# A graph network on one core: the attention of layer 2 is turned back a slot earlier, and its denominators by transposes

## The chip, the cores and the metric

The kernel runs on one core of a Trainium2 chip. A core has five engines that work through queues of their own: TensorE (PE; its weight loads are shown as PEld), VectorE (DVE), ScalarE (ACT), GpSimd (POOL) and SyncE (SP), which issues most of the transfers. Engines wait for each other by semaphores, and an instruction that waits holds up everything behind it on its engine. TensorE writes its results to PSUM, a small memory of banks; another engine must read a bank before TensorE may use it for something else. The metric is the device time of one execution in microseconds (us). Three runs of the kernel before took 2074.66, 2077.97 and 2079.85 us; the median is 2077.97.

## What is computed

Four layers of graph network over 32 graphs of 512 nodes with 64 features. All graphs share one adjacency matrix `adj`. Each layer normalizes, applies a relu, and adds its output to its input:

```python
h = jnp.maximum(_layernorm(x, axis=-1), 0.0)
x = x + _L0_gnn_ref(h, adj, w_self, w_neighbor, bias)   # h W + (adj h) W' + b
h = jnp.maximum(_layernorm(x, axis=-1), 0.0)
x = x + _L1_gnn_ref(h, 0, net_params, adj)              # twice: relu((adj z) W_i)
h = jnp.maximum(_layernorm(x, axis=-1), 0.0)
x = x + _L2_gnn_ref(h, adj, W, a)                       # attention, below
h = jnp.maximum(_layernorm(x, axis=-1), 0.0)
x = x + _L3_gnn_ref(h, adj, Wh, bh, W_out, b_out)       # eight heads and an output attention
```

The change is in layer 2, a graph attention:

```python
Wh = jnp.einsum('bnf,of->bno', h, W)
e = jax.nn.leaky_relu((Wh @ a[:F])[:, :, None] + (Wh @ a[F:])[:, None, :], negative_slope=0.2)
att = jax.nn.softmax(jnp.where(adj[None] > 0, e, NEG), axis=-1)
return jax.nn.elu(jnp.einsum('bij,bjo->bio', att, Wh))
```

## The kernel before

The batch is worked on in 16 pairs of graphs. A pair's values stand as 128 partitions by 512 elements: four blocks `c` of 128 nodes, two graphs `k`, 64 features. Layers 0 to 2 form the first stage, up to about 487 us; the rest of the time is layer 3, whose work is laid out in periods by `flow_period` and which the change leaves as it is, but for what the drain (below) runs ahead of it.

**Slots.** The first stage is a software pipeline written out by hand. `slot(k)` issues, for k from 0 to 16, layer 0 of pair k, layer 1 of pair k-2 and k-3, the preparation of layer 2 for pair k-4 and its attention for pair k-5 (the object `u`, of class `Gat`). The order of the calls is the order of the instructions on TensorE, VectorE and ScalarE, inside `tc.manual_schedule`. Within a slot, as it stands before the change:

- POOL adds the bias to x of pair k (L1122). ScalarE copies `nt1b`, a sum over neighbours that TensorE left in PSUM at the end of the slot before (`copied`, L928).
- VectorE adds `po0`, the projection of layer 0, to x (L1129) and centres the result for the next norm (`centre`: mean L861, L862, difference L863); ScalarE squares it (L881).
- TensorE sums over neighbours for layer 1 (`nt1`, L921) and transposes for the attention (`ht2`, L310); ScalarE copies both. VectorE makes half of the attention's scores (L1005). TensorE projects `nt1b` (`po1b`, L941), VectorE adds it with a relu (L1108).
- TensorE transposes (`ht0`) and sums (`nt0`) for layer 0, VectorE centres once more and makes the other half of the scores, TensorE projects `po1a` and prepares the next attention (`wh`, L967, and two `e1`, L974, whose exps into `c` are L990).
- A third centring; four variances (L899); TensorE multiplies the scores with the values, `acc` (L1018) and `den` (L1027), the latter as sums in 128 rows; ScalarE takes the roots (L906) and copies `acc` and `den` to SBUF, tile `kept` (L1037). VectorE weighs the next values (L995), takes reciprocals (L914) and finishes three norms (relu, L885).
- TensorE projects layer 0 (`po0`, L941) and sums over neighbours of `z` (L921, left in PSUM for the next slot). Then comes whatever `begun` has for this slot (`more`): in slots 6, 8, 10 and 12 the row checks `judge_rows` on VectorE (L201 to L213), in slot 15 `judge` (L240 to L244), which turns a column by TensorE.
- The end of the attention, `u.end()`: `read` multiplies `kept` with `pick`, a matrix of 128 x 2 that adds up two rows out of four sets (`den_ps`, L1049), turns the attention back by four transposes (`op_ps`, L1055), takes the reciprocal (L1060) and the product (L1062). `rest` takes the exp (L1070), adds into x (L1073, L1074), centres, and squares (L1076). Its variance is summed in the next slot (list `ended`).

The trace drops the digits of tile names: `nt0`, `nt1` and `nt1b` evacuate tiles that are all called `nt_ps`, and `ht0` and `ht2` both appear as `ht`.

ScalarE loads a table when it goes from a root to an exp or back (ACT_TABLE_LOAD). The load stands directly before the first instruction that needs it.

**Banks.** The first stage has three PSUM pools: `ps_t` with four buffers (neighbour sums, transposes, `wh`, `e1`, and before the change `op_ps` and `fill_ps`), `ps_o` with two (`po0`, `po1a`, `po1b`) and `ps_g` with two (`acc`, `den`, `den_ps`).

**The drain.** `drain` finishes the last four attentions, g2, g1, g0 and `last`, when no layer 0 is left to work beside them. `fill(n)` multiplies n times something that nobody reads. Before `last.scores(1)` it runs nine periods of `flow_period` ahead, which prepare layer 3's first features on ScalarE, transpose them (`hx_ps`) and multiply (`g_ps`).

Of the kernel before, what the change touches and what calls it, by code (L numbers as in the profile page):

```python
# [8 lines left out]
F32 = mybir.dt.float32  # L9
# [13 lines left out]
def fast_form(  # L23
# [818 lines left out]
    with (  # L842
# [107 lines left out]
        class Gat:  # L950
# [92 lines left out]

            def read(self):
                acc, tot = self.kept
                den = ps_g.tile([P, N], F32, name="den_ps", tag="acc")
                den = den[:, : 2 * C].rearrange("p (c k) -> p c k", k=2)
                for c in range(C):
                    nc.tensor.matmul(  # L1049
                        den[:, c], lhsT=tot[:, c * P : (c + 1) * P], rhs=pick,  # L1050
                        start=True, stop=True,
                    )
                op = ps_t.tile([P, C, 2, F], F32, name="op_ps", tag="ps")
                for c in range(C):
                    nc.tensor.transpose(  # L1055
                        op[:, c].rearrange("p k f -> p (k f)"), acc[:, c * P : (c + 1) * P],
                        ident,
                    )
                rec = tiny.tile([P, 2, C], F32, name="rec")
                nc.vector.reciprocal(rec.rearrange("p k c -> p c k"), den)  # L1060
                self.sq = o = work.tile([P, 2, C, F], F32, name="o")
                nc.vector.tensor_tensor(  # L1062
                    o, op.rearrange("p c k f -> p k c f"),
                    rec[:, :, :, None].to_broadcast([P, 2, C, F]), OP.mult,
                )
# [13 lines left out]
        n0, n1, n2, gat = {}, {}, {}, {}  # L1079
        ended = []  # L1080
        nt1b, z, po0 = {}, {}, {}
# [36 lines left out]
        def slot(k, more):  # L1118
# [15 lines left out]
            if n:  # L1134
                n.a()
                n.square()
                some.append(n)
            if l1:
                h = n1.pop(k - 2).h
                nt1 = copied(neighbours(lambda c: h[:, c]), "nt1")  # L1140
# [47 lines left out]
            if l0:  # L1188
                po0[k] = project([(ht0, ws2), (nt0, wn2)], "po0")
            if l1:  # L1190
                nt1b[k - 2] = neighbours(lambda c: z[:, c, :])
            if more:
                more()
            if u:
                u.end()

        def fill(n):


            p = ps_t.tile([P, N], F32, name="fill_ps", tag="ps")  # L1200
            for i in range(n):
                nc.tensor.matmul(p, lhsT=ident, rhs=adj_t[:, 0, :], start=True, stop=True)

        def drain():


            g2, g1, g0 = gat.pop(M - 4), Gat(M - 3, n2.pop(M - 3).h), None
            nt1b[M - 2] = copied(nt1b[M - 2], "nt1b")
            h = n1.pop(M - 1).h
            nt1 = copied(neighbours(lambda c: h[:, c]), "nt1")  # L1210
# [27 lines left out]
            g1.scores(0)  # L1238
            g0.flip()
            g2.read()  # L1240
            g1.scores(1)
# [12 lines left out]
            g2.rest()  # L1254
            g0.scores(0)
            g1.read()
            last.prepare()
# [7 lines left out]
            s = Spread()  # L1265
            s.add(g2)
            for i in range(-10, -1):
                flow_period(i)
            g0.read()
            last.scores(1)  # L1270
# [3 lines left out]
            g0.rest()  # L1274
            s.add(g1)
            last.read()
            last.rest()
# [9 lines left out]
        mask_t = setup.tile([P, C, N], F32, name="mask", tag="raw")  # L1287
        pick = setup.tile([P, 2], F32, name="pick")

        def edges():  # L1290
            nc.vector.tensor_scalar(mask_t, adj_t, 0.0, None, op0=OP.is_gt)
            nc.vector.tensor_tensor(
                pick, ident[:, 0::F], ident[:, 32::F], OP.add
            )

# [611 lines left out]
```

## Time and profile before

| | |
|---|---|
| runs | 2074.66, 2077.97, 2079.85 us; median 2077.97 |
| profiled execution | 2077.38 us, span 2075.5 us, mean granted clock 0.985 |
| TensorE busy | 1984.1 us (96%) |
| VectorE busy | 1746.2 us (84%) |
| ScalarE busy | 1319.3 us (64%) |
| POOL busy | 1446.3 us (70%) |
| slots 6 to 16 | 107.35 to 387.73 us |
| drain | 387.73 to about 487 us |

Times in the timeline are counted from the start of the span. A line of a timeline gives the start, the length, the engine, the source line, the instruction, what it writes and reads, and how many alike were merged; in brackets stands the idle time of the engine before it and what ended it. A line of a window gives the stretch, its length, then for TensorE, its weight loads, VectorE, ScalarE and POOL the busy time and the number of instructions, and then the clock that TensorE was granted (1.00 is full speed), the share of the transfers and GB/s. A matmul of float32 appears as two instructions, a transpose as one. Matmuls are pipelined, so the lengths of groups overlap a little; in the chain of waits, each step has only the time that it adds.

### The profile page before, as it was taken

The numbers are of one execution on the slowest core, as the hardware profiler recorded it, in microseconds if no ns is written. First come the engines' busy times: TensorE is split into PE (matmuls) and PEld (weight loads), VectorE is DVE, ScalarE is ACT, GpSimd is POOL, SyncE is SP. The second block draws the span as 40 slices with busy tenths as digits, with TensorE's granted clock in tenths as the row PEclk, the third lists the DMA queues.
The fourth block names the chain that finished last, engine by engine and source line by source line (L and its number), as shares of the span: only waits on it lengthen the run. The fifth ranks groups of instructions, "written<-read, shape, count | busy, mean of one in ns | idle before, by whom it ended". The sixth has DMA issues, their size and how long they took to land.

```text
span 2075.5 us, 29392 instructions
## 1 busy us (share of the span) xinstructions
PE 1984.1 (96%) x9438; PEld 744.5 (36%) x9438; DVE 1746.2 (84%) x4087; ACT 1319.3 (64%) x2008; POOL 1446.3 (70%) x834
## 2 busy tenths in 40 slices
PE   7999999877999999999999999999999999999995
PEld 4555555422333333333333333333333333333332
DVE  6688887647888998988888889888888888889994
ACT  3444444343676777677777777777777777776674
POOL 2000000002888999898989899998888988888996
PEclk9999999978999999999999999999999999999998
DMA  4000000000222223233323233232333233222233
GB/s 121 1 1 1 1 1 1 1 0 21 78 78 74 83 70 84 76 83 77 79 76 77 76 84 82 75 84 68 78 77 74 70 77 76 75 71 78 76 83 79
DMA packets 185875, 128.05 MB, mean 62 GB/s; under 512 B 124984, under 2 KB 130272, under 8 KB 185584
## 3 DMA queue, kind: packets, MB, share of 16 engines
q1 hardware_dynamic: 166480, 125.30, 22.9%
q10 hardware_dynamic: 18720, 0.59, 0.5%
q8 instruction: 76, 1.25, 0.3%
q14 instruction: 87, 0.71, 0.1%
q0 software_dynamic: 512, 0.20, 0.1%
HBM read 119.48 MB, written 5.37 MB: 60 GB/s over the span
## 4 chain that ended last, share of the span: by engine, by line
PE 78%; DVE 11%; POOL 5%; ACT 3%; DMA 2%; issue 2%; ACTq 0%; SPq 0%; DVEq 0%; POOLq 0%
PE s_ps L383 23%; PE av L438 21%; PE tot_ps L450 6%; PE y_ps L568 5%; PE gT_ps L613 5%; PE nt_ps L921 5%; POOL p_att L416 3%; PE g_ps L550 3%; PE acc L1018 2%; DVE s L1005 2%; PE den L1027 1%; DVE mean L861 1%; PE hx_ps L310 1%; PE po L941 1%; DVE p_att L395 1%
## 5 line engine op out<-in xcount | busy, mean ns | idle before, releaser
L416 POOL TENSOR_TENSOR p_att<-p_att,topb 128x1024 f32<-128x1024 f32 x429 | 1008.4, 2385 | 0.0
L395 DVE CUSTOM_DVE_ANT_0 p_att<-s_ps,flow_neg 128x512 f32<-128x512 f32 x1152 | 726.0, 686 | 100.0 <-PE s_ps L383 98.2
L383 PE MATMUL s_ps<-g,hx 64*128 64x512 f32 x2048 | 515.1, 614 | 14.0 <-DVE p_att L432 11.4
L420 POOL TENSOR_TENSOR p_att<-p_att,topb 128x512 f32<-128x512 f32 x286 | 360.7, 1284 | 170.9 <-DMA topb<-top_row 130.7
L429 ACT ACTIVATE p_att<-p_att 128x1024 f32<-128x1024 f32 x288 | 304.7, 1058 | 157.3 <-POOL p_att L420 77.0
L432 DVE TENSOR_TENSOR p_att<-e_ps,p_att 128x1024 f32<-128x1024 f32 x288 | 337.9, 1197 | 29.1 <-ACT e_ps L429 27.4
L429 ACT ACTIVATE e_ps<-p_att 128x1024 f32<-128x1024 f32 x288 | 292.6, 1029 | 74.0 <-POOL p_att L416 62.2
L383 PEld LDWEIGHTS s_ps<-g,hx 64*128 64x128 f32 x2048 | 174.9, 186 | 326.1 <-DVE top L395 174.8
L438 PE MATMUL av<-p_att,hd 128*64 128x512 f32 x1024 | 269.7, 605 | 0.2
L438 PE MATMUL av<-p_att,hn 128*64 128x512 f32 x1024 | 263.3, 592 | 0.0
L1122 POOL TENSOR_TENSOR x<-x,bias_b 128x512 f32<-128x512 f32 x16 | 20.4, 1279 | 296.1 <-DVE hn L863 296.1
L586 DVE SCALAR_TENSOR_TENSOR cat<-y_ps,bh,cat 128x512 f32<-128x512 f32 x256 | 180.1, 745 | 17.0 <-ACT cat L578 15.4
L562 ACT COPY g<-g_ps 128x512 f32<-128x512 f32 x128 | 131.8, 1138 | 91.3 <-PE g_ps L550 91.1
L578 ACT ACTIVATE cat<-y_ps,bh 128x512 f32<-128x512 f32 x256 | 161.3, 681 | 35.5 <-PE y_ps L568 35.2
L450 PE MATMUL tot_ps<-p_att,ones 128*32 128x512 f32 x1152 | 156.4, 608 | 3.7 <-DVE p_att L432 3.7
L568 PE MATMUL y_ps<-o_att,wh_sb 64*128 64x512 f32 x512 | 137.0, 594 | 0.0
L613 PE MATMUL gT_ps<-cat,wo_sb 128*64 128x512 f32 x512 | 131.6, 592 | 0.0
L438 PEld LDWEIGHTS av<-p_att,hn 128*64 128x64 f32 x1024 | 73.8, 137 | 146.0 <-issue 146.0
L438 PEld LDWEIGHTS av<-p_att,hd 128*64 128x64 f32 x1024 | 62.3, 136 | 165.5 <-issue 132.6
L921 PE MATMUL nt_ps<-adj_t,hn 128*128 128x512 f32 x256 | 117.0, 600 | 0.8 <-DVE hn L885 0.8
L487 DVE TENSOR_TENSOR o_att<-av,recb 128x512 f32<-128x512 f32 x144 | 99.1, 688 | 19.3 <-DMA recb<-rec_row 16.0
L528 POOL TENSOR_TENSOR hd<-hn 128x128 f32<-128x128 f32 x32 | 15.6, 487 | 138.5 <-ACT hn L519 138.5
(192 smaller groups left out, 2196.6 us busy)
## 6 DMA issues: line engine op xcount, KB each, us to landing
topb<-top_row SPq DMA_DIRECT2D x288, 256.0 KB
recb<-rec_row SPq DMA_DIRECT2D x288, 128.0 KB
out_dram<-y SPq DMA_DIRECT2D x32, 128.0 KB
x<-in_x_dram SPq DMA_DIRECT2D x3, 1024.0 KB
top_row<-top SPq DMA_DIRECT2D x144, 4.0 KB
parts<-tot SPq DMA_DIRECT2D x144, 4.0 KB
parts<-tot ACTq DMA_DIRECT2D x144, 4.0 KB
rec_row<-rec_flow SPq DMA_DIRECT2D x144, 4.0 KB
```

The lines of the kernel that those rows point to most:

```text
L383: nc.tensor.matmul(ps[:, k], lhsT=x[halves(k), r * P : (r + 1) * P], rhs=g[halves(k), :], start=True, stop=True,)
L395: nc.vector.tensor_tensor_reduce(out=self.p[r][:, k], in0=ps[:, k], in1=flow_neg[:, r], scale=-1.0, scalar=BIG, op0=OP.add, op1=OP.min, ac ...
L416: engine.tensor_tensor(self.p[r], self.p[r], self.topb, OP.subtract)
L420: engine.tensor_tensor(p, p, self.topb[:, k], OP.subtract)
L429: nc.scalar.activation(to, self.p[r], AF.Exp, scale=-1.0)
L432: nc.vector.tensor_tensor(self.p[r], self.joined, self.p[r - 1], OP.add)
L438: nc.tensor.matmul(self.av[halves(k), :], lhsT=self.v(k, j) if j % 2 else self.less_next(k, j), rhs=self.p[j][:, k], start=(j == 0), stop= ...
L450: nc.tensor.matmul(ps[q : q + 32, :], lhsT=ones, rhs=self.p[2 * e + 1][:, k], start=True, stop=True,)
L568: nc.tensor.matmul(ps, lhsT=wh_sb[halves(k), 2 * self.i + k, :], rhs=self.o[halves(k), :], start=True, stop=True,)
L586: nc.vector.scalar_tensor_tensor(self.cat[:, k], self.y[k], bh[:, h : h + 1], self.cat[:, k], op0=OP.add, op1=OP.max,)
L613: nc.tensor.matmul(self.gps[halves(k), :], lhsT=wo_sb[:, h, :], rhs=Heads.cat.pop((self.b + k, h)), start=(h == 0), stop=(h == H - 1),)
L921: nc.tensor.matmul(p, lhsT=lhs(k), rhs=adj_t[:, k, :], start=(k == 0), stop=(k == C - 1))
```

## The change

`read` is split. A new method `back` does its work on TensorE: four transposes of the denominators (instead of four multiplications with `pick`) into `den_ps`, four of the attention into `op_ps`. `read` keeps the work of VectorE; since a transposed column holds each sum 32 times, it picks one of 32 and adds the two sets with a reduction, ahead of the reciprocal. In a slot, `back` is called directly behind the projection `po0`, ahead of the neighbour sums of `z`, and `end` (`read` and `rest`) is called in the next slot, behind the first centring and square. `op_ps` and `fill_ps` take their buffers from `ps_o` instead of `ps_t`. In the drain, `back` is called before each `read`, and for g0 both are called before the nine periods of `flow_period` instead of behind them.

```diff
-            def read(self):
+            def back(self):
                 acc, tot = self.kept
                 den = ps_g.tile([P, N], F32, name="den_ps", tag="acc")
-                den = den[:, : 2 * C].rearrange("p (c k) -> p c k", k=2)
                 for c in range(C):
-                    nc.tensor.matmul(
-                        den[:, c], lhsT=tot[:, c * P : (c + 1) * P], rhs=pick,
-                        start=True, stop=True,
+                    nc.tensor.transpose(
+                        den[:, c * P : (c + 1) * P], tot[:, c * P : (c + 1) * P], ident
                     )
-                op = ps_t.tile([P, C, 2, F], F32, name="op_ps", tag="ps")
+                op = ps_o.tile([P, C, 2, F], F32, name="op_ps", tag="po")
                 for c in range(C):
                     nc.tensor.transpose(
                         op[:, c].rearrange("p k f -> p (k f)"), acc[:, c * P : (c + 1) * P],
                         ident,
                     )
+                self.op, self.den = op, den
+
+            def read(self):
+                op, den = self.op, self.den
                 rec = tiny.tile([P, 2, C], F32, name="rec")
-                nc.vector.reciprocal(rec.rearrange("p k c -> p c k"), den)
+                den = den.rearrange("p (c k e r) -> p k c e r", c=C, k=2, e=2)
+                nc.vector.tensor_reduce(rec, den[:, :, :, :, 0], AX.X, OP.add)
+                nc.vector.reciprocal(rec, rec)
...
@@ slot @@
                 n.square()
                 some.append(n)
+            while turned:
+                turned.pop().end()
...
                 po0[k] = project([(ht0, ws2), (nt0, wn2)], "po0")
+            if u:
+                u.back()
+                turned.append(u)
             if l1:
                 nt1b[k - 2] = neighbours(lambda c: z[:, c, :])
             if more:
                 more()
-            if u:
-                u.end()
 
         def fill(n):
-            p = ps_t.tile([P, N], F32, name="fill_ps", tag="ps")
+            p = ps_o.tile([P, C, 2, F], F32, name="fill_ps", tag="po")
...
@@ drain @@
             nt1b[M - 2] = copied(nt1b[M - 2], "nt1b")
+            turned.pop().end()
...
+            g2.back()
             g2.read()
...
+            g1.back()
             g1.read()
...
             s.add(g2)
+            g0.back()
+            g0.read()
             for i in range(-10, -1):
                 flow_period(i)
-            g0.read()
             last.scores(1)
...
+            last.back()
             last.read()
```

`pick` and the instruction that made it are gone.

## The prediction

> **What bounds the kernel now.** I read the page's head and chain first, then the timeline of the three busy engines over one slot of the layer-0-to-2 stage, then the timeline of the drain, then the granted clock in 2 us windows.
>
> The page's head and its chain of waits:
>
> ```profile
> span 2075.5 us, 29392 instructions
> PE 1984.1 (96%) x9438; PEld 744.5 (36%) x9438; DVE 1746.2 (84%) x4087; ACT 1319.3 (64%) x2008; POOL 1446.3 (70%) x834
> PE 78%; DVE 11%; POOL 5%; ACT 3%; DMA 2%; issue 2%; ACTq 0%; SPq 0%; DVEq 0%; POOLq 0%
> ```
>
> From about 487 us on TensorE is the bound, and the change touches nothing there. Everything turns on the first 487 us, so the shares over the span say nothing. One slot there, on TensorE, VectorE and ScalarE (start, length, engine, line, instruction; in brackets the idle time before it and what ended it):
>
> ```profile
> 310.52 3.60 PE L921 MATMUL nt_ps<-adj_t,z 128*128 128x512 f32 x8
> 313.96 0.95 PE L1049 MATMUL den_ps<-pick,kept 128*128 128x2 f32 x8
> 314.77 0.63 PE L1055 MATMUL op_ps<-ident,kept 128*128 128x128 f32 x4
> 320.49 1.16 PE L941 MATMUL po1b<-wl,nt1b 128*128 128x128 f32 x8 [1.22 <-ACT nt1b L928]
> ...
> 314.94 0.21 DVE L1060 RECIPROCAL rec<-den_ps 128x8 f32<-128x8 f32 x1 [4.45 <-PE den_ps L1049]
> 315.44 0.69 DVE L1062 TENSOR_TENSOR o<-op_ps,rec 128x512 f32<-128x512 f32 x1 [0.28 <-PE op_ps L1055]
> 318.61 0.69 DVE L863 TENSOR_TENSOR o<-x,mean 128x512 f32<-128x512 f32 x1
> ...
> 309.38 1.28 ACT L1070 ACT_TABLE_LOAD   x1
> 316.16 0.63 ACT L1070 ACTIVATE e<-o 128x512 f32<-128x512 f32 x1 [5.50 <-DVE o L1062]
> 319.33 0.63 ACT L1076 ACTIVATE o<-o 128x512 f32<-128x512 f32 x1 [2.54 <-DVE o L863]
> 319.87 0.57 ACT L928 COPY nt1b<-nt_ps 128x512 f32<-128x512 f32 x1
> ```
>
> This is a ring. VectorE idles 4.45 us for `den_ps`, which stands behind `nt_ps<-z` on TensorE. Its five instructions of L1062 to L863 run 315.44 to 319.30; the square (L1076) follows; the `nt1b` copy stands behind the square on ScalarE's queue; `po1b` waits for the copy; from 320.49 TensorE works without a gap up to the next `op_ps`, 20.55 us. 20.55 + 5.07 = 25.62 us a slot. TensorE itself is busy 24.38 of them. Slots 6, 8, 10 and 12 end with row checks (L201 to L213) that run 284.36 to 289.59, 5.2 us of VectorE; they fit into the 4.45 us of idle but for 0.4. So two slots take 51.7 us.
>
> The drain, and the clock:
>
> ```profile
> 400.03 5.40 PE L921 MATMUL nt_ps<-adj_t,z 128*128 128x512 f32 x8 [1.93 <-ACT c L990]
> 418.01 2.07 PE L974 MATMUL e_ps<-ht,wa 64*128 64x512 f32 x2 [0.41 <-DVE o L1062]
> 437.65 1.81 PE L974 MATMUL e_ps<-ht,wa 64*128 64x512 f32 x2 [3.04 <-ACT c L990]
> 439.61 5.82 PE L1202 MATMUL fill_ps<-adj_t,ident 128*128 128x512 f32 x7
> 463.10 2.21 PE L310 MATMUL hx_ps<-ident,hs 128*128 128x128 f32 x8 [10.09 <-ACT hs L524]
> 467.98 1.86 PE L1049 MATMUL den_ps<-pick,kept 128*128 128x2 f32 x8
> ...
> 412.00:414.00 2.00, 1.67 (x16) 1.43 (x14) 1.90 (x5) 0.00 (x0) 0.00 (x0) 1.00 0.00 0
> 414.00:416.00 2.00, 0.42 (x8) 0.42 (x8) 2.00 (x4) 1.56 (x3) 0.00 (x0) 1.00 0.00 0
> 418.00:420.00 2.00, 1.99 (x2) 0.50 (x2) 2.00 (x4) 0.24 (x1) 0.00 (x0) 0.50 0.01 4
> ```
>
> `e_ps` waits 3.04 us for a bank, and `fill_ps` after it starts with VectorE's L1062 (438.86 to 439.55); both wait for buffers of the pool that also holds `op_ps`. Idles of 1.9 us (413.7 to 415.6) and 1.93 us (398.1 to 400.0) are each followed by a clock of 0.50, while the 1.66 us idle before `po1b` in the slots with row checks left it at 1.00.
>
> **The change, part by part.** T is the end of `nt_ps<-z` of the slot before; the times are laid end to end from the rows above and the like rows of that slot.
>
> *The matmuls of `pick`.* Eight passes, 0.79 us in the chain, become four transposes, priced like `op_ps` in the chain, 0.51 for four: -0.3 us a unit. Both sets now stand before `nt_ps<-z`, so TensorE needs 24.38 - 0.3 = 24.1 us a slot.
>
> *The extra reduction.* The nearest rows are L467 (128x8 from 128x16, 0.17 us) and L243 (from PSUM, 0.28). I take 0.2. In a slot VectorE then waits for the exp, which hides it; only the last unit pays it.
>
> *The move in an ordinary slot.* `po0` ends at T-4.4, VectorE's relu at T-4.2. The add of `po0`, mean, mean and difference run to T-1.9, the reduction, reciprocal, product and L1073 to T. Now the exp: on ScalarE it stands behind the `nt1b` copy (T to T+0.6), the square (to T+1.1) and its table load, which ran in an idle stretch before (309.38) and now runs behind the square, 1.28 us, to T+2.4; the exp ends at T+3.0. Behind it VectorE waits, and with it all its queue: L1074, means and difference to T+5.4, four scores to T+8.1, `po1b`'s two adds, means and difference to T+10.4. ScalarE's next square and the `nt0` copy end at T+11.5. The second `e1` matmul needs that copy for its bank and is reached by TensorE at T+11.3 (nt 3.44, ht 0.44, po1b 0.89, ht 0.44, nt 3.44, po1a 0.89, wh 1.04, e1 0.72). So the new chain just fits: 24.2 us, -1.4 against 25.62. Queued behind the exp on ScalarE are the square, the `nt1` and both `ht` copies; they end by T+7.6, and `po1a` wants `nt1` at T+8.6. The move issues no DMA and passes nothing on SP; POOL's bias add is ready some 7 us before its reader.
>
> *The move behind row checks.* The 5.2 us now have only T-4.2 to T before them and end at T+1.0. The add of `po0` starts there, the product ends at T+4.4, table load and exp at T+5.7, the difference at T+8.1, the scores at T+10.8, the second difference at T+13.1, the `nt0` copy at T+14.2. TensorE, at its second `e1` since T+11.8 (`po1a` too waits 0.4), idles 2.3 us, and a restart costs 0.3 (the first `po1b` above takes 1.16 us, in the chain 0.89): slots 7, 9, 11 and 13 take 26.7 us.
>
> *Slot 16.* VectorE waits in slot 15 for `own_ps` behind `nt_ps<-z` (365.21, hidden until now behind the same wait as `den_ps`). So it is as late, `nt1`'s copy stands behind the late square, `po1a` idles 3.9 us: 24.3 us against 22.2.
>
> *Sum of slots 6 to 16:* from `den_ps` at 107.35 to that at 387.73 are 280.4 us. After: 6 x 24.2 + 4 x 26.7 + 24.3 = 276.3, -4.1 us.
>
> *The clock.* The new idles of 2.3 and 3.9 us are longer than those that lost it. A loss costs 1.5 (`nt_ps` 5.11 us at 83.3 against 3.60) to 3.1 us (6.2 us at half from 418.0). Below: nothing, where the 2.3 us fall across two stretches. I take 2.2, midway, in three of the four slots, and in slot 16: +8.8. Slots: +4.7.
>
> On this the Trainium skill (TensorE: Matmul & The Clock Gate, "Why this matters for your kernels") advises against idle gaps above about 3 us. By it only slot 16 would lose the clock, and the total would be 6.6 us lower; the rows with 1.9 us decide.
>
> The Trainium skill speaks against the change in another place: ScalarE: Activation LUTs, "What ACT_TABLE_LOAD costs", puts a switch at 1.28 us for the load and 1.38 for a drain. By that the chain in every slot would be 1.4 us longer and the ordinary slot would gain nothing. Here the load at 431.69 is followed by the exp at 432.98 with nothing between, so 1.28 stands.
>
> *The drain.* (a) `nt_ps` at 400.03: its chain through the late exp gives about T+12.0 for T+12.4: -0.3. (b) `e_ps` at 418.01 no longer waits for L1062, and starts with the clock still up: -1.2. (c) `op_ps` and `fill_ps` leave `e_ps`'s pool: the wait of 3.04 and that for L1062 go, six fills run behind `e_ps` from 434.7, at full clock 5.2 us, to 439.9. Late next are the scores on VectorE (the last ends at 442.1, with the reduction 442.3): the last `acc` matmul and `den` (0.45 + 1.85) end at 444.7 for 453.06: -8.3. What hides it is nothing: after it comes a chain of single steps to 463.10. (d) The `den_ps` and `op_ps` at 467.98, 2.75 us to 470.8, move into the idle 10.09 us before 463.10: -2.75; I put back 0.4, since the clock at 0.50 until 475 may now reach into `acc`. (e) The last reduction +0.2. Sum -12.0; between -7 (the fills of (c) at half clock, 10 us) and -14 (`acc` in (b) and `nt_ps` in (a) at full clock).
>
> *Total:* 4.7 - 12.0 = -7.3. The profiled execution took 2077.38 us (2075.5 and 1.9 around it), 0.6 below the median of the runs, 2077.97. So 2070.1, and against the median 2070.7: I say 2070.5.
>
> **Rivals.** (R1) The clock holds through the stalls. For it: 1.66 us held. Against: 1.9 did not. Slots -4.1, drain -12.0: 2062.
>
> (R2) Slower: the half clock does not come back in the stalled slots. The work behind the second `e1` is half-width scores, `acc` and `den`; after 437.85 and 463.1 the clock took 7 and 12 us. Five places at p us each against 4.1 + 12.0: from p = 3.2 us on it is slower; with all of `acc`, `den` and `po0` at half (p about 7) 2097; at p = 4.6, midway, 2085. Against it: the time at half from 83 and from 400.3 was 3.4 us.
>
> (R3) The drain pays half: the fills run cold as they do now (439.61: 0.83 us each), and the late clock meets `acc`. -5 with slots +4.7: 2078.
>
> (R4) The change does not open the ring, since the exp is still behind other work. Then slots keep 51.7 us a pair: about 2066 with the drain alone.
>
> **How the numbers follow.** Likeliest case 0.46, with its own range 2066 to 2076; R1 0.18, R2 0.16, R3 0.14, R4 0.06. What a measurement can tell is 0.3%, 6.2 us: faster means below 2071.7, slower above 2084.2. Faster: 0.28 of the likeliest, all of R1, 0.05 of R4: 0.51. Slower: 0.11 of R2, 0.03 of R3, 0.01 of the likeliest: 0.15. Same: the other 0.34. The range takes in R1's centre and R2's turning point and a little more: 2060 to 2084.
>
> **What will show it.** Right: `po1b` without the 1.22 us idle; VectorE idle before L1078 by some 3 us, released by the exp; a table load behind the square; idle before `e_ps` behind row checks of about 2.3 us with a clock below 1.00 after it; the six fills starting right behind `e_ps`. Wrong: an ordinary slot above 24.5 us, a clock of 1.00 in slots 7 to 13, fills that still wait, or a start of the attention stage that moved by less than 3 us.

## The result and the profile after

The changed kernel took 2077.49 us (median of 12 runs, 2073.82 to 2080.06), the kernel before, on the same chip, 2077.55 (2074.66 to 2080.31). The ratio is 0.9999, with a 95% interval of 0.999 to 1.0008: no difference. One execution among the experiments (the exp behind the copy) took 2447.42 us at a mean granted clock of 0.781, where its four others had 0.980 to 0.985, and is left out of that kernel's ratio. The profiled execution took 2077.25 us, with a span of 2075.3 us and a mean clock of 0.981 (before: 2077.38, 2075.5, 0.985). The head and the chain of waits of the page after:

```profile
span 2075.3 us, 29298 instructions
PE 1984.9 (96%) x9374; PEld 738.2 (36%) x9374; DVE 1748.6 (84%) x4102; ACT 1320.3 (64%) x2008; POOL 1445.5 (70%) x834
PE 60%; POOL 6%; DMA 4%; DVE 3%; issue 1%; ACT 1%; SPq 0%; ACTq 0%; POOLq 0%; DVEq 0%
```

TensorE's total is as good as unchanged, and nothing in it says that the first 487 us were rearranged. The reading starts from the slots. The starts of the last neighbour sum of a slot, `nt_ps<-z`, give the length of each slot:

| slot | 6 | 7 | 8 | 9 | 10 | 11 | 12 | 13 | 14 | 15 | 16 | sum |
|---|---|---|---|---|---|---|---|---|---|---|---|---|
| before | 25.63 | 26.07 | 25.62 | 26.07 | 25.63 | 26.06 | 25.63 | 26.06 | 25.62 | 25.63 | 22.25 | 280.3 |
| after | 24.54 | 28.71 | 24.54 | 29.89 | 24.54 | 29.99 | 24.54 | 30.03 | 24.54 | 24.53 | 26.06 | 291.9 |

The ordinary slots became 1.1 us shorter. The four that follow row checks became 2.6 to 4.0 us longer, slot 16 by 3.8. Against that, the drain, from `nt_ps<-z` of slot 16 to the add behind the exp of g0, went from 98.4 to 80.8 us.

The changed kernel's timeline of TensorE, first a slot behind row checks (293.40 to 323.43), then an ordinary one:

```profile
308.18 1.07 PE L974 MATMUL e_ps<-ht,wa 64*128 64x512 f32 x2
311.18 2.07 PE L974 MATMUL e_ps<-ht,wa 64*128 64x512 f32 x2 [1.93 <-ACT nt L928]
313.18 5.71 PE L1018 MATMUL acc<-s,v 128*64 128x512 f32 x16
...
323.43 3.60 PE L921 MATMUL nt_ps<-adj_t,z 128*128 128x512 f32 x8
...
330.74 1.06 PE L941 MATMUL po1b<-wl,nt1b 128*128 128x128 f32 x8
...
337.43 1.07 PE L974 MATMUL e_ps<-ht,wa 64*128 64x512 f32 x2
338.71 1.12 PE L974 MATMUL e_ps<-ht,wa 64*128 64x512 f32 x2 [0.21 <-ACT nt L928]
339.77 3.65 PE L1018 MATMUL acc<-s,v 128*64 128x512 f32 x16
```

In the ordinary slot `po1b` (330.74) no longer waits. In its place the second `e_ps` waits for the `nt0` copy: 0.21 us. Behind row checks it waits 1.93 us, and what follows runs at half clock: the second `e_ps` takes 2.07 us for 1.12, `acc` 5.71 for 3.65.

VectorE and ScalarE of the same two slots, from the timelines of each engine:

```profile
297.58 0.68 DVE L1133 TENSOR_TENSOR x<-x,po 128x512 f32<-128x512 f32 x1
302.61 0.69 DVE L1078 SCALAR_TENSOR_TENSOR x<-e,x 128x512 f32<-128x512 f32 x1 [0.86 <-ACT e L1074]
...
322.83 0.69 DVE L1133 TENSOR_TENSOR x<-x,po 128x512 f32<-128x512 f32 x1 [3.30 <-PE po L941]
326.32 0.69 DVE L1077 SCALAR_TENSOR_TENSOR x<-o,x 128x512 f32<-128x512 f32 x1
330.15 0.69 DVE L1078 SCALAR_TENSOR_TENSOR x<-e,x 128x512 f32<-128x512 f32 x1 [3.14 <-ACT e L1074]
```

```profile
327.06 0.58 ACT L928 COPY nt1b<-nt_ps 128x512 f32<-128x512 f32 x1 [5.67 <-PE nt_ps L921]
327.55 0.63 ACT L881 ACTIVATE sq<-hn 128x512 f32<-128x512 f32 x1
328.20 1.28 ACT L1074 ACT_TABLE_LOAD   x1
329.49 0.63 ACT L1074 ACTIVATE e<-o 128x512 f32<-128x512 f32 x1
```

In the ordinary slot VectorE is done with L1077 at 327.0 and then waits 3.14 us for the exp. ScalarE has been idle for 5.67 us by then, but the `nt1b` copy, which waits for TensorE's last sums, stands ahead of the exp in its queue, and so do the square and the table load. Behind row checks VectorE starts at 297.58, 0.75 us after the end of those sums and not 4.0 us before it, as in the ordinary slot, and all that it does for TensorE comes later.

The drain, in TensorE's timeline of the changed kernel:

```profile
414.22 3.70 PE L921 MATMUL nt_ps<-adj_t,z 128*128 128x512 f32 x8 [2.82 <-ACT c L990]
428.09 1.11 PE L967 MATMUL wh_ps<-wgv,ht 64*128 64x65 f32 x16 [2.33 <-ACT ht L312]
...
430.04 2.84 PE L1210 MATMUL fill_ps<-adj_t,ident 128*128 128x512 f32 x6
...
442.00 5.42 PE L1210 MATMUL fill_ps<-adj_t,ident 128*128 128x512 f32 x12
```

The twelve instructions of `fill_ps` at 442.00 start right behind `e_ps` and take 5.42 us; before, they started after a wait of 3.04 us and ran cold. `nt_ps` takes 3.70 us for 5.40, and the six fills at 430.04 take 2.84: in this execution the clock was kept, although the waits ahead of them are long (2.82 us, before the change 1.93, and 2.33). In the second profile of the changed kernel (below) it was lost at this `nt_ps`, which took 6.55 us behind the same wait. Layer 3's first L395 starts at 487.12 us, 2.85 us earlier than before.

### The profile page after: what moved, and what is told of

It reads as the page before. It is cut to its first block, busy times and chain, and to the rows that moved or that the text cites. A ratio compares the mean times of both kernels' runs of the same rounds, so it can differ in the third digit from the quotient of the medians.

```text
span 2075.3 us, 29298 instructions
## 1 busy us (share of the span) xinstructions
PE 1984.9 (96%) x9374; PEld 738.2 (36%) x9374; DVE 1748.6 (84%) x4102; ACT 1320.3 (64%) x2008; POOL 1445.5 (70%) x834
## 4 chain that ended last, share of the span: by engine, by line
PE 60%; POOL 6%; DMA 4%; DVE 3%; issue 1%; ACT 1%; SPq 0%; ACTq 0%; POOLq 0%; DVEq 0%
PE s_ps L383 21%; PE av L438 20%; PE tot_ps L450 6%; PE y_ps L568 5%; POOL p_att L416 5%; PE gT_ps L613 5%; PE g_ps L550 3%; DMA topb<-top_row 2%; DVE p_att L395 2%; POOL p_att L420 1%; DVE p_att L432 1%; DMA top_row<-top 1%; PE hx_ps L310 1%; ACT e_ps L429 1%; DMA recb<-rec_row 0%
## 5 line engine op out<-in xcount | busy, mean ns | idle before, releaser
L395 DVE CUSTOM_DVE_ANT_0 p_att<-s_ps,flow_neg 128x512 f32<-128x512 f32 x1152 | 726.0, 685 | 96.5 <-PE s_ps L383 95.4
```

The source lines that it names most:

```text
L395: nc.vector.tensor_tensor_reduce(out=self.p[r][:, k], in0=ps[:, k], in1=flow_neg[:, r], scale=-1.0, scalar=BIG, op0=OP.add, op1=OP.min, ac ...
```

## The experiments

The theory: the drain's gain is real, and the slots give it back, because behind row checks VectorE is late, the second `e_ps` then waits for a bank that the late `nt0` copy frees, and the short idle costs clock on top. The rivals: the exp with its table load makes the slots long by itself; the drain did not pay; layer 3 takes back any lead. In all tables "drain" is the stretch from `nt_ps<-z` of slot 16 to the add behind the exp of g0, and each ratio is to the kernel before on the same chip (medians 2077.55 to 2080.77 us).

### Without the row checks

```diff
-            for c in range(C):
-                begun[6 + 2 * c] = lambda c=c: judge_rows(c)
+            nc.vector.memset(sound[:, 2 + C : 2 + 2 * C], 1.0)
```

> The changed kernel without the row checks (L201 to L213) in slots 6, 8, 10 and 12: the four columns of their verdict are set to 1, so part of the test of the input is left out. Theory (late VectorE): the checks push the start of VectorE's chain to the end of the slot; slots 7, 9, 11 and 13, 28.71 to 30.03 us in the changed kernel, then take the 24.54 of the others, and slot 16 keeps its 26.06. Slots 6 to 16 go from 291.9 to about 271.4 us, the total from 2077.5 to about 2057. Rival (the exp and its table load in the chain make the slots long by themselves): the four slots stay over 27 us and the total over 2070.

2059.72 us, 0.990 (0.988 to 0.992). Slots 6 to 15 all take 24.53 or 24.54 us, slot 16 25.8; together 271.2. So the row checks make the four slots long, all 20.5 us of it, and the exp and its table load alone do not. What remains in every slot is the wait of 0.21 us before the second `e_ps`.

### The drain alone, and the slots alone

The drain's part, put into the kernel before:

```diff
-                op = ps_t.tile([P, C, 2, F], F32, name="op_ps", tag="ps")
+                op = ps_o.tile([P, C, 2, F], F32, name="op_ps", tag="po")
...
-            p = ps_t.tile([P, N], F32, name="fill_ps", tag="ps")
+            p = ps_o.tile([P, C, 2, F], F32, name="fill_ps", tag="po")
...
+            g0.read()
             for i in range(-10, -1):
                 flow_period(i)
-            g0.read()
```

> The kernel before, with the drain's part of the change alone: op_ps and fill_ps in the other pool, the last but one unit read ahead of the flow periods; slots, exp and the matmuls of pick as before. Theory (the drain's gain is real and is lost again in the slots): slots 6 to 16 stay at 280.3 us, the stretch from the last nt_ps<-z of slot 16 to L1074 behind the exp of the last but one unit goes from 98.4 to some 83 to 87 us, the total from 2077.5 to 2064 (2061 to 2068). Rival 1 (the drain pays half, the fills run cold): 2072. Rival 2 (layer 3 takes back any lead, as it took the 2.85 us of the changed kernel): 2077.

The slots' part is the changed kernel with these edits taken back in the drain (`op_ps` stays in `ps_o` within the slots and goes back to `ps_t` in the drain):

```diff
-            p = ps_o.tile([P, C, 2, F], F32, name="fill_ps", tag="po")
+            p = ps_t.tile([P, N], F32, name="fill_ps", tag="ps")
...
-            g0.back()
-            g0.read()
             for i in range(-10, -1):
                 flow_period(i)
+            g0.back()
+            g0.read()
```

> The changed kernel with the slots' part alone: op_ps goes to the other pool in the slots only, fill_ps stays in the pool of e_ps, the last but one unit is turned and read behind the flow periods. Theory (slots cost, drain pays): slots 6 to 16 take 290 to 292 us as in the changed kernel, against 280.3 before; the drain keeps its waits of about 3 us before e_ps and its cold fills; total 2086 to 2090. Rival (the slots cost little, and the gain of the drain went elsewhere): total 2076 to 2080.

| | slots 6 to 16 | drain | first L395 | time, ratio |
|---|---|---|---|---|
| before | 280.3 | 98.4 | 490.0 | 1 |
| drain alone | 280.3 | 79.8 | 469.9 | 2062.06, 0.992 (0.9903 to 0.9938) |
| slots alone | 291.9 | 94.4 | 499.3 | 2090.9, 1.0053 (1.0036 to 1.0071) |
| both | 291.9 | 80.8 | 487.1 | 2077.49, 0.9999 (0.999 to 1.0008) |

Each half does about what it was expected to do: the drain alone brings 18.2 us, the slots alone cost 10.7. They do not simply add up, since that would leave a gain of 7.5 us where the two together showed 0.1. The profiles show 5 us of the difference: the slots' part alone shortens the drain by 4.0 us already (98.4 to 94.4), and both parts together gain 17.6 us there where the drain alone gains 18.7. What is left of it is within what layer 3 and the first 107 us vary by (both kernels again, below). How much of the drain's gain is clock can be read from the records of the granted clock: from 400 to 476 us the kernel before has 34 us at half clock in four places, the drain alone 10 us in one (442.4 to 452.6).

### The clock: TensorE kept busy through the stall

```diff
                 for k in range(2):
+                    if k and warm:
+                        fill(2)
                     nc.tensor.matmul(
                         e1[k], lhsT=wa1[halves(k), :], rhs=self.ht[halves(k), :],
...
```

`warm` is set in slots 7, 9, 11 and 13.

> The changed kernel with two more matmuls (fill_ps, 128x512, 0.87 us each) ahead of the second e_ps in slots 7, 9, 11 and 13; they stand where TensorE otherwise waits 1.92 us for the copy of nt0. Theory (the short idle costs its own 2 us and then a half clock behind it): the clock stays at 1.00 from slot 6 to 14, the second e_ps in these slots takes 1.1 us and not 2.07, acc 3.65 and not 5.71; the four slots go from 28.71 to 30.03 us to 26.5 to 27.0, slots 6 to 16 from 291.9 to about 279.5, the total falls by 11 to 13 us to some 2065. Rival (the half clock has another cause than this idle): the four slots stay at 28.7 to 30 us.

2068.37 us, 0.9946 (0.9931 to 0.9961). The four slots take 27.03 us each, slots 6 to 16 281.4. TensorE's timeline of this kernel, the slot behind row checks:

```profile
298.70 1.07 PE L976 MATMUL e_ps<-ht,wa 64*128 64x512 f32 x2
299.70 1.98 PE L1212 MATMUL fill_ps<-adj_t,ident 128*128 128x512 f32 x4
301.70 1.12 PE L976 MATMUL e_ps<-ht,wa 64*128 64x512 f32 x2
302.75 3.65 PE L1020 MATMUL acc<-s,v 128*64 128x512 f32 x16
```

The matmuls between the two `e_ps` do nothing useful, and yet the slot is 1.7 to 3.0 us shorter than in the changed kernel. That separates the two parts of the loss. Of 28.71 to 30.03 us, the wait is 27.03 - 24.54 = 2.5 us in each slot, and the half clock behind it is 1.7, 2.9, 3.0 and 3.0.

### The denominators by transposes alone

The kernel before with `back`'s four transposes and the reduction in `read`, and nothing else of the change:

```diff
                 for c in range(C):
-                    nc.tensor.matmul(
-                        den[:, c], lhsT=tot[:, c * P : (c + 1) * P], rhs=pick,
-                        start=True, stop=True,
+                    nc.tensor.transpose(
+                        den[:, c * P : (c + 1) * P], tot[:, c * P : (c + 1) * P], ident
                     )
...
```

> The kernel before with one part of the change alone: the denominators by four transposes and a reduction in place of the eight matmuls of pick; slots, pools and drain as before. Theory (the place holds 0.8 us of TensorE, the transposes 0.45 to 0.5, and the ring of the ordinary slot holds both): the ordinary slot falls from 25.63 to about 25.3 us, plus 0.2 for the reduction, slots 6 to 16 from 280.3 to 278 to 281 us, the total by 0 to 3 us. Rival (the parts of the change that cost time are the transposes and the reduction): slots 6 to 16 at 285 us or more.

The ordinary slot took 25.31 us, as expected. Yet the sum is 284.3 us, and the time 2082.65 us, 1.001 (1.0001 to 1.002): a little slower, not faster. TensorE's timeline shows what was left out of the expectation, here behind row checks:

```profile
296.68 1.16 PE L941 MATMUL po1b<-wl,nt1b 128*128 128x128 f32 x8 [2.27 <-ACT nt1b L928]
...
298.43 4.97 PE L921 MATMUL nt_ps<-adj_t,hn 128*128 128x512 f32 x8
```

Behind row checks VectorE cannot start earlier, so what TensorE saves it waits longer for `nt1b`: 2.27 us in this slot. In three of the four slots that cost the clock (27.43, 27.29 and 27.44 us; the fourth 26.27), and slot 16 went from 22.25 to 23.72. The time saved on TensorE became idle time: with 1.66 us of it, in the kernel before, these slots kept the clock, and with 2.27 us they lost it three times out of four.

### The place of the exp

Two orders of the same work were run. In the first, VectorE's `read` and the exp are issued ahead of the centring and the square of n1, but behind the `nt1b` copy. In the second the exp is ahead of the copy too. `exp` is the exp and L1077, `gain` is L1078 and what follows it in `rest`. The diff is that of the second order; the first leaves the copy where it was:

```diff
-            if k - 3 in nt1b:
-                nt1b[k - 3] = copied(nt1b[k - 3], "nt1b")
...
+            for t in turned:
+                t.read()
+                t.exp()
+            if k - 3 in nt1b:
+                nt1b[k - 3] = copied(nt1b[k - 3], "nt1b")
             some = []
             n = make(n1, k - 1)
...
             while turned:
-                turned.pop().end()
+                turned.pop().gain()
```

> The changed kernel with half of what the run with the exp ahead changed: the turned unit is read ahead of the centring of n1 on VectorE and its exp issued ahead of the square on ScalarE, but behind the nt1b copy. Theory (the exp's place behind the square and the centring of n1 ahead of it are most of the loss, the copy costs 0.6 to 1.9 more): L1078 starts 0.7 us earlier in an ordinary slot, some 23.8 us, and 1.0 us earlier behind row checks, some 25.4 us with the clock kept; slots 6 to 16 268 to 274 us, total 22 us below the kernel before (18 to 25). Rival (the nt1b copy, which waits for the last matmuls of the slot before, is what holds the exp): 24.5 us and over 27 us behind row checks, total within 10 us of the kernel before.

> The changed kernel with another order on two engines: the turned unit is read and its exp issued ahead of the nt1b copy and of n1's square on ScalarE, and VectorE takes the centring of n1 while the exp runs. Theory (the place of the exp on ScalarE behind the nt1b copy, which waits for the last matmuls of the slot before, and its table load set the chain): the wait before L1078 (3.14 us in an ordinary slot) falls below 0.5, VectorE gets 3 us ahead and the row checks fit into its idle time: all slots 24.1 to 24.6 us, slots 6 to 16 266 to 273 us, total 2052 to 2059. Rival (the exp is not what holds, row checks alone do): slots 7, 9, 11 and 13 stay at 27 to 30 us, total 2072 to 2078.

| | ordinary slot | behind row checks | slots 6 to 16 | ratio |
|---|---|---|---|---|
| after | 24.54 | 28.71 to 30.03 | 291.9 | 0.9999 |
| exp behind the copy | 24.01 | 27.60 to 27.65 | 278.0 | 0.9964 (0.9949 to 0.9978) |
| exp ahead of the copy | 23.21 | 24.72 | 264.2 | 0.9859 (0.9839 to 0.988) |

With the exp ahead of the copy, the run did what was expected: 2051.77 us. The other order was expected to bring 22 us and brought 7.5. I had reckoned the wait behind row checks at 0.9 us; it was 1.63 us, and that still lost the clock in each of the four slots:

```profile
299.41 1.78 PE L974 MATMUL e_ps<-ht,wa 64*128 64x512 f32 x2 [1.63 <-ACT nt L928]
301.13 4.64 PE L1018 MATMUL acc<-s,v 128*64 128x512 f32 x16
```

Behind row checks and in the total this is what the rival had said (over 27 us, within 10 us of the kernel before). So the copy was a large part of what held the exp: of the 29 us that both steps bring, 7.5 come without moving the exp ahead of it. In the two profiled executions each step takes 14 us off the slots (291.9, 278.0, 264.2); what each is worth in the total depends on how often the clock is lost, and that varies. ScalarE and VectorE with the exp ahead of the copy, in an ordinary slot:

```profile
317.80 1.28 ACT L1078 ACT_TABLE_LOAD   x1
321.05 0.63 ACT L1078 ACTIVATE e<-o 128x512 f32<-128x512 f32 x1 [1.97 <-DVE o L1066]
323.45 0.58 ACT L928 COPY nt1b<-nt_ps 128x512 f32<-128x512 f32 x1 [1.77 <-PE nt_ps L921]
```

```profile
321.05 0.69 DVE L1080 SCALAR_TENSOR_TENSOR x<-o,x 128x512 f32<-128x512 f32 x1
321.66 0.68 DVE L861 TENSOR_REDUCE mean<-x 128x8 f32<-128x512 f32 x1
...
323.19 0.68 DVE L1084 SCALAR_TENSOR_TENSOR x<-e,x 128x512 f32<-128x512 f32 x1
```

The table load now lies in an idle stretch (317.80), the exp starts with its input, VectorE centres n1 meanwhile, and the add behind the exp (L1078 in the changed kernel, L1084 here) starts at 323.19 without a wait, at the end of TensorE's last sums and not 3.3 us behind it. VectorE gets far enough ahead in the ordinary slots that most of the 5.2 us of row checks fit into its idle time.

### The bank of the second `e_ps`

The changed kernel with one buffer moved, in the slots only:

```diff
-            def prepare(self):
+            def prepare(self, second=(ps_t, "ps")):
...
-                e1 = [ps_t.tile([P, N], F32, name="e1_ps", tag="ps") for k in range(2)]
+                e1 = [
+                    p.tile([P, N], F32, name="e1_ps", tag=t)
+                    for p, t in ((ps_t, "ps"), second)
+                ]
...
-                gat[k - 4].prepare()
+                gat[k - 4].prepare((ps_o, "po"))
```

> The changed kernel with one buffer moved: in the slots the second e_ps takes its bank from the pool of po and op_ps, so that it waits for VectorE's po1b adds and not for ScalarE's copy of nt0; nothing else differs. Theory (in the changed kernel this bank is what holds TensorE, in the ordinary slot too, where the wait of 0.21 us also splits the four matmuls of e_ps, 2.34 us for 1.01): the ordinary slot falls from 24.54 to 23.2 to 23.7 us, the slots behind row checks from 28.71 to 30.03 us to 24.2 to 26 us with the clock at 1.00, slots 6 to 16 to 264 to 272 us, the total to 20 to 27 us below the kernel before. Rival (VectorE's queue is late as a whole, so acc waits for the scores in place of e_ps for the bank): the slots behind row checks keep 27 us or more, the total within 10 us of the kernel before.

2060.12 us, 0.9898 (0.988 to 0.9915). The ordinary slot is 23.21 us, the four others 26.75 to 26.94, slots 6 to 16 273.7, and the total 20.7 us less than that of the kernel before. TensorE's timeline of this kernel, behind row checks and then in an ordinary slot:

```profile
292.31 1.16 PE L941 MATMUL po1a<-wl,nt 128*128 128x128 f32 x8 [1.83 <-ACT nt L928]
...
294.34 1.27 PE L977 MATMUL e_ps<-ht,wa 64*128 64x512 f32 x4
...
296.80 3.65 PE L1021 MATMUL acc<-s,v 128*64 128x512 f32 x14 [0.19 <-DVE s L1008]
...
318.99 1.08 PE L977 MATMUL e_ps<-ht,wa 64*128 64x512 f32 x4
320.00 3.65 PE L1021 MATMUL acc<-s,v 128*64 128x512 f32 x16
```

In the ordinary slot the bank was what held TensorE in the changed kernel: without it the slot takes 23.21 us. Behind row checks it was not all. There the wait has moved ahead, to `po1a`, which waits 1.83 us for the `nt1` copy: neither what the theory nor what the rival named, and these slots take 0.8 us more than expected. They are only 0.1 to 0.3 us below the 27.03 us that the changed kernel's slots take with the stall filled; the rest of their gain is clock, which was lost in one of the four.

### The verdict's reduction, and all together

Slot 16 stayed longer than the 22.25 us of the kernel before in all the kernels with the slots' part: 25.8 to 27.25 us, and 23.38 with the exp behind the copy. In slot 15 VectorE waits for `own_ps` (L243), and the work of slot 16 starts late behind it. VectorE in the changed kernel:

```profile
376.25 0.28 DVE L243 TENSOR_REDUCE unsound<-own_ps 1x1 f32<-1x128 f32 x1 [7.41 <-PE own_ps L242]
```

In the kernel with the exp ahead of the copy, L243 was moved behind the add of the turned unit:

```diff
         nc.tensor.transpose(ps, own, ident)
-        nc.vector.tensor_reduce(unsound, ps, AX.X, OP.min)
+        told.append(ps)
+
+    told = []
+
+    def tell():
+        nc.vector.tensor_reduce(unsound, told.pop(), AX.X, OP.min)
         nc.vector.tensor_scalar(unsound, unsound, 0.0, None, op0=OP.is_equal)
...
                 turned.pop().gain()
+            while told:
+                tell()
```

> The run with the exp ahead, and VectorE's last reduction of the verdict on the input (L243, which waits for own_ps behind the last matmuls of slot 15) put behind the gain of the turned unit in the next slot. Theory (in slot 16 VectorE starts 3.4 us late behind this wait, po1a then idles 3.07 us and the clock falls to 0.50 for 10.2 us): the wait of 7.26 us before L243 goes, slot 16 falls from 26.09 to 21.5 to 23 us, the total by 3 to 5 us against the run with the exp ahead, to about 31 to 33 us below the kernel before. Rival (slot 16 is short of work for TensorE and idles anyway): slot 16 stays above 25 us.

2045.39 us, 0.9836 (0.9822 to 0.9849). Slot 16 falls from 26.09 to 18.90 us, more than expected. With the bank of the second `e_ps` moved as well:

> The run with the exp ahead and the verdict's reduction later, and the second e_ps with its bank from the other pool in the slots. Theory (with the exp ahead only the bank still splits e_ps behind row checks, 0.39 us of wait and 1.1 of lost overlap): the four slots behind row checks fall from 24.72 to about 23.2 us, slots 6 to 16 by 6 us from 257 to 251, the total to some 40 us below the kernel before. Rival (VectorE's own 5.2 us of checks hold these slots): they stay at 24 us or more, the total at 35 us below.

2041.26 us, 0.9809 (0.9796 to 0.9823), 39.5 us less than the kernel before. The four slots take 23.21 to 23.54 us, slots 6 to 16 251.9. In TensorE's timeline of a slot behind row checks no wait of more than 0.15 us is left; only `acc` runs a little longer than elsewhere (3.98 us for 3.65), behind the scores:

```profile
282.87 1.11 PE L972 MATMUL wh_ps<-wgv,ht 64*128 64x65 f32 x16
283.81 1.08 PE L982 MATMUL e_ps<-ht,wa 64*128 64x512 f32 x4
284.82 3.98 PE L1026 MATMUL acc<-s,v 128*64 128x512 f32 x16
```

This version beats both kernels, and it is the change under study with the exp, one wait and one bank put in another place.

### Both kernels again

> The changed kernel once more, for a second profile of it beside the kernel before. Theory (the 2.85 us by which layer 3 started earlier in its first profile are within what the first 107 us and layer 3 vary from run to run): slots 6 to 16 take 291 to 293 us and the drain 80 to 82 as in the first profile; layer 3 takes 1588 to 1592 us as in all profiles but the first one of the kernel before (1585.5); total within 3 us of the kernel before. Rival (layer 3 runs longer behind the changed drain): layer 3 of the second profile of the kernel before stays at 1586 or below.

> The kernel before once more, for a second profile. Theory (its first profile had a short layer 3 by chance): layer 3, from the first L395 to the end, takes 1588 to 1592 us, slots 6 to 16 280.3 us and the drain 96 to 99 us. Rival (layer 3 behind the old drain is shorter by itself): 1584 to 1587 us.

| | slots 6 to 16 | drain | first L395 | layer 3 |
|---|---|---|---|---|
| before | 280.3 | 98.4 | 489.97 | 1585.5 |
| before, again | 280.3 | 98.6 | 492.00 | 1589.0 |
| after | 291.9 | 80.8 | 487.12 | 1588.2 |
| after, again | 287.9 | 84.1 | 483.83 | 1589.9 |

The changed kernel took 2077.94 us this time, 0.9991 (0.9981 to 1.0); the one profiled execution of the kernel before took 2082.87 us. Its slots and its drain did not repeat as I expected: in the second profile one of the four long slots kept its clock (27.02 us), and the drain lost it in one place more. The kernel before, which loses no clock in its slots and loses it at the same four places of the drain, repeats to 0.2 us in both stretches, and its layer 3 took 1589.0 us, within what the theory said. Averaged over both profiles, layer 3 starts 5.5 us earlier in the changed kernel, and the whole kernel takes 0 to 3 us less. Layer 3 takes back some of it: 1585.5 to 1589.0 us in the three profiles of kernels that still have `pick`, 1588.2 to 1592.4 (mean 1590.7) in the eleven of kernels with the transposes. The code of layer 3 is the same in all; why it should run 2 to 3 us longer, or whether three profiles only happened to be short, stays open.

## Why the prediction was right and wrong

The predicted 2070.5 us missed by 7, and the range of the likeliest case, 2066 to 2076, missed too; the time fell into the wide range only. In number it is closest to R3, but not by its mechanism. Two of the prediction's own signs of being wrong came, both narrowly: an ordinary slot above 24.5 us (24.54), and a start of the attention stage that moved by less than 3 us (2.85 in the first pair of profiles; 8.17 in the second). By the steps:

- **The ordinary slot**, 24.2 us, was 24.54, and the reason given was wrong. The step "TensorE needs 24.38 - 0.3 = 24.1 us a slot" took the busy time before as TensorE's need. The need is 23.21 us (exp ahead, and the bank). The rest is the pair of `e_ps`: 1.01 us to the start of `acc` when nothing stands between them, 2.34 when a wait of 0.21 us does. The new ring through the exp and the `nt0` copy still bounded the slot; it did not "just fit". The prediction's own sum had the copy 0.2 us behind TensorE (T+11.5 and T+11.3); what it put at nothing is what so short a wait does to the overlap, 1.33 us. A part of that was lost in the kernel before already, where the four took 1.60 us in a slot and 1.08 in the drain:

```profile
327.29 1.60 PE L974 MATMUL e_ps<-ht,wa 64*128 64x512 f32 x4
...
397.02 1.08 PE L974 MATMUL e_ps<-ht,wa 64*128 64x512 f32 x4
```

- **Behind row checks** the step was right in kind and in size: 24.2 to 26.7 us without clock loss was predicted, 24.54 to 27.03 measured, 2.5 us in both. The place, the second `e1`, was right too.
- **The clock** is the term that was mis-sized. The prediction took "2.2, midway, in three of the four slots, and in slot 16: +8.8". In the first profile it was 1.7 + 2.9 + 3.0 + 3.0 in the four slots and, if all that slot 16 took above the predicted 24.3 us is clock, 26.06 - 24.3 = 1.8 there: +12.3. In the second profile it was 1.6 + 0 + 1.7 + 3.2 + 1.8 = 8.3. So the value was fair for one execution and 3.5 us short for another: this term varies from run to run. Of the 6.9 us between the +4.7 predicted for the slots and the +11.6 of the first profile, 3.5 are this; the other 3.4 are ten times 0.34 from the ordinary slot.
- The rule weighed against it, from the Trainium skill (TensorE: Matmul & The Clock Gate, "Why this matters for your kernels"), would have left the four slots at full clock. In seven of the eight waits of 1.92 us, over the two profiles, it was lost. The row with 1.9 us had decided rightly.
- **The table load** stood behind the square as predicted (328.20), cost 1.28 us, and was followed by the exp with nothing between. The exp ended at T+3.1 for a predicted T+3.0.
- **The drain**, -12.0 us predicted, brought -17.6 and -14.5 in the two profiles, with a part that belongs elsewhere: 1.3 us of `den_ps` and `op_ps` moved from its head into slot 16, and 0.9 us of the like came into slot 5. Steps (c) and (d) came as worked out: no wait before `e_ps`, fills at full clock, `acc` limited by the scores. The rest of the surplus, in the first profile, is the clock kept at `nt_ps` of (a) and behind `e_ps` of (b), named as the end of the range and not taken; in the second profile it was lost at (a). "R3, the drain pays half" fell with it.
- **R2** fell as a mechanism (the half clock came back within 3.4 to 6.8 us each time). Its price "from p = 3.2 us a place" was nearly reached all the same, by 1.7 to 3.0 us a place in the first profile and 3.2 in one place of the second.
- **R1** (the clock holds) came true behind row checks in one slot out of eight. **R4**, held least likely, is nearest for the slots: its reason, that the exp is still behind other work, is what the run with the exp ahead shows, and without the clock losses a pair of slots takes 24.54 + 27.03 = 51.57 us, for the 51.7 that it said. Over such a pair the move by itself gained 0.1 us.

Summed up: in the first pair of profiles the slots are 6.9 us worse than predicted and the drain 5.6 better, in the second 2.9 worse and 2.5 better. So slots and drain together changed by -6.0 and -6.9 us, near the predicted -7.3; that is luck, since the two errors cancel. The total missed by what the prediction put at nothing outside them. In the first pair, whose two executions lie near the medians of their kernels, 2.9 us were lost ahead of slot 6 (0.9 in slot 5, the rest with one clock loss more) and 2.7 in layer 3, where "the change touches nothing": together they take back nearly all of the 6.0. In the second pair the same two terms were -1.5 and +0.9. The first varies from run to run; of the second no run shows the cause. The signs of both halves were argued rightly; the balance of two large terms was not to be had to 0.3% while one of them depends on whether a 2 us idle loses the clock.

## What to carry to other kernels

When work is moved into the next step of a pipeline, ask for each instruction what stands ahead of it in its own engine's queue and what that waits for: here an exp that could have started at once stood behind a copy that waited for the last matmuls, and putting it ahead was worth some 26 us, where the change as it was made brought nothing that could be measured. A stall of 2 us on TensorE should be priced with the half clock that may follow, as an addition that comes or not from run to run; filling it with useless matmuls is the experiment that tells the two apart. And if a large change moves nothing, run its halves: -18 and +11 us are two results, not none.

## What the runs showed of the hardware

**Two matmuls on 64 rows run beside each other, if nothing comes between them.** The four instructions of `e_ps` (64x512 each) take 1.08 us together, and 1.07 and 1.12 us one behind the other when the second pair waits, be it for 0.21 us. The Trainium skill (TensorEngine Tiling (Array Packing), "Theoretical Speedup") gives up to twofold for a small dimension of at most 64; 1.08 for 2.19 agrees, and shows what a wait in between costs.

**The granted clock changes on a grid of 3.41 us.** All its changes within a profile lie on one grid of that length, in all 14 profiles. The Trainium skill (TensorE: Matmul & The Clock Gate, "What's actually happening") tells of a window of about 3.4 us that runs on its own; the grid agrees. The same wait of 1.92 us, before the same instruction, in two slots of one execution of the changed kernel (the second profile), as windows laid on the grid:

```profile
195.00:198.42 3.42, 2.71 (x25) 1.76 (x24) 3.32 (x8) 0.53 (x2) 0.00 (x0) 1.00 0.02 5
198.42:201.83 3.41, 2.20 (x8) 0.78 (x10) 3.38 (x6) 3.05 (x9) 0.00 (x0) 1.00 0.00 0
201.83:205.24 3.41, 3.41 (x24) 0.95 (x24) 3.38 (x8) 2.18 (x4) 1.28 (x1) 1.00 0.00 0
...
246.20:249.62 3.42, 3.06 (x26) 2.11 (x26) 3.32 (x8) 0.88 (x2) 0.00 (x0) 1.00 0.02 5
249.62:253.03 3.41, 1.85 (x6) 0.64 (x8) 3.41 (x6) 3.00 (x9) 0.00 (x0) 1.00 0.01 2
253.03:256.44 3.41, 3.41 (x10) 0.97 (x8) 3.34 (x8) 1.96 (x3) 1.27 (x1) 0.50 0.00 0
```

In the first slot the idle falls across two stretches (TensorE busy 2.71 and 2.20 us), and the clock stays at 1.00. In the second nearly all of it falls into one (1.85 us), and the next has 0.50. The idle of 2.82 us in the drain of the changed kernel was split as well:

```profile
409.50:412.91 3.41, 1.90 (x20) 1.07 (x20) 3.31 (x8) 0.81 (x2) 0.00 (x0) 1.00 0.00 0
412.91:416.33 3.42, 2.11 (x5) 1.06 (x6) 3.42 (x7) 3.34 (x9) 0.00 (x0) 1.00 0.01 2
416.33:419.74 3.41, 3.41 (x14) 1.13 (x14) 1.15 (x4) 0.58 (x1) 0.00 (x0) 1.00 0.00 0
```

Over the first 530 us of all 14 profiles, of the stretches at full clock with TensorE busy for less than 40%, all 54 were followed by half clock; from 40 to 55%, 23 of 53; from 55 to 70%, 11 of 104; above, 6 of 1714. The busy share of one stretch is therefore not the whole rule, since from 40 to 55% both happen about equally often. Nor is the length of the idle: 1.66 us before `po1b` was kept in all eight slots behind row checks of the two profiles of the kernel before, and 1.63 us before the second `e_ps` was lost in all four with the exp behind the copy. What else counts was not tried.
